# Where the squares go in a pairwise-product kernel: difference-0 products in the shared tiles, 32 separate products of difference 32, and a q sum that accumulates onto a copy

## The chip, the cores and the metric

The kernel runs on one core of one Trainium2 chip. The metric is the device time of one execution in microseconds (us). All arithmetic is float32.

## The reference, cut to what matters

x has 1024 batch rows, 64 fields and 16 embedding columns. Three layers each multiply every field of x with every row of a running h, and contract the 64 x 64 products with weights:

```python
x0 = h = x; xs = []
for i in range(3):
    z = einsum('bfe,bge->bfge', x0, h).reshape(B, 64 * 64, 16)
    y = einsum('oc,bce->boe', W[i], z) + b[i]          # 128 outputs
    x_i, h = (y[:, :64], y[:, 64:]) if i < 2 else (y, y)
    xs.append(x_i)
out = sum(concat(xs, 1), axis=2) @ fc_w.T + fc_b       # (1024, 1)
```

In layer 0 h is x itself, so the products are symmetric. Only pooled sums leave layers 1 and 2. The kernel therefore forms from the unordered products x_f x_g two results of 64 rows each: h (the lower half of layer 0's output) and q (a weight combination that the kernel derives from W1, W2 and fc). The output is the sum over embedding columns of h times q, plus terms linear in x.

## The kernel before, in words

The batch is cut into 32 chunks of 32 rows; a chunk is 64 fields x 512 columns (32 rows x 16). TensorE contracts tiles of 128 products x 512 columns against 64 weight columns, so that a matmul fills one half of the array's columns ("128*64" in the profile) and two of them, one in each column half, run side by side. A float32 matmul of the program is two MATMUL records in the trace, called two passes here.

The unordered products of a chunk fill 16 tiles of 128 rows. With 16 tiles there are 2048 products. Before, these are the differences g - f = 1 to 32 (modulo 64); each product of difference 32 then occurs twice and half of them get weight zero. The 64 squares are not in the tiles. They are in a tile `e` of 128 rows per chunk: x in its upper half (a load, `load_e`), x squared in its lower half (ScalarE, `square`). From it come four more matmuls for a chunk pair's two q sums and two h sums and two for the linear term y:

- `q_extra` (L585): 128 rows, weights `va` or `vb` (linear term above, squares below), one for each chunk.
- `h_extra` (L589): 64 rows (the squares) against `w0ds`, one for each chunk.
- `v0x` (L596): 64 rows (x) against `v0`, one for each chunk.

Six chunks are done plainly at the start and the end. The other 26 form 13 pairs (chunks a and b of pair k). A pair needs 7 instead of 8 contractions of 8 tiles per half because sums and differences of the tiles are formed on VectorE and GpSimd first (`w_product`, `w_both`, `w_mix`; tiles X, T2, T3, B21, B22) and combined weights `ws` are used: 56 matmuls for a pair. Their sums lie in PSUM tiles `alpha`, `beta`, `gamma`, `delta` of 512 columns; each uses one half of the partitions (`p["A"]` or `p["O"]`). `alpha` holds first the common part p1, of which `snap_p1` (L682, ScalarE) keeps a copy in SBUF, and goes on to h and q parts. `w_qa` (L696, VectorE) adds that copy to the separately summed `beta`; `w_hb`, `w_ha`, `w_uu` then form h times q, one half of the partitions at a time.

The order of the work is written out by hand: `at(when, fn)` records a job under a nominal time, the jobs are sorted by it, and each engine executes its own in that order. One nominal unit stands for two matmuls side by side (a slot). A pair's window is 31 units long (`SPAN`). Odd windows (`a_leads`, L807) and even ones (`o_leads`, L821) alternate; a window's `window(...)` zips two columns of jobs, one for each half of the array's columns. `first_window` is the first pair's. In odd windows `joint_squares` (L747) issues all h and y extras of two pairs as eight 64-row matmuls, which occupy the four quarters of the array ("64*64"); the two `q_extra` of a pair stand in the zipped columns (`first_fill`, `late_run`). `end_pair` records VectorE's closing work. The last two chunks, 2 and 3, are contracted in two cuts of 384 and 128 columns (`end_q`, `end_extra`).

SyncE issues the loads in the same order (`load_pair`). Copies into the two PSUM banks tagged `y` (`second`, L568, ScalarE) feed VectorE's products, bank by bank in turn.

Of the kernel before, what the change touches and what calls it, by code (L numbers as in the profile page):

```python
# [42 lines left out]
F = 64  # L43
# [15 lines left out]
NV = 196  # L59
SQ = slice(96, 128)  # L60
# [10 lines left out]
def cin_kernel(ctx, tc, xra, xrb, wh, w0r, w1h, w2t, wx1, wx0, vec, lin, out):  # L71
# [7 lines left out]
    halves = [slice(0, F), slice(F, 128)]  # L79

# [23 lines left out]
    fcb, w0ds, fcr = vs[:, 3:4], vs[:, 4:68], vs[:, 68:196]  # L104

    misc = ps.tile([128, N], F32, tag="acc", name="misc", bufs=4)
# [22 lines left out]
    va, vb, v0 = (const_tile(n, [128, F]) for n in ("va", "vb", "v0"))  # L129
# [6 lines left out]
    xas, xbs, xxs, es = {}, {}, {}, {}  # L136
# [22 lines left out]
    def load_e(c):  # L159
        es[c] = sp.tile([128, N], F32, tag="e", name=f"e_{c}", bufs=4)  # L160
        nc.sync.dma_start(out=es[c][halves[0]], in_=xra[c, 0:F])

    def load_xx(k):
        xxs[k] = sp.tile([128, N], F32, tag="xx", name=f"xx_{k}")
        for n in range(2):
            nc.sync.dma_start(out=xxs[k][halves[n]], in_=xra[2 * k + n, 0:F])

    def copy_x(c):
        k, h, x = c // 2, halves[c % 2], xas[c][:, 0, :]
        if k not in xxs:  # L170
            xxs[k] = sp.tile([128, N], F32, tag="xx", name=f"xx_{k}")
        es[c] = sp.tile([128, N], F32, tag="e", name=f"e_{c}", bufs=4)
        nc.scalar.activation(es[c][halves[1]], x[halves[1]], AF.Square)
        nc.scalar.copy(es[c][halves[0]], x[halves[0]])
        nc.scalar.copy(xxs[k][h], x[h])

    def square(c):
        nc.scalar.activation(es[c][halves[1]], es[c][halves[0]], AF.Square)
# [32 lines left out]
    def shifted(c, j, tag):  # L211
        xbs.setdefault(c, {})[j] = ps.tile(
            [128, N], F32, tag=tag, name=f"xp_{c}_{j}", bufs=4 if tag == "acc" else 2
        )

    def shift_pair(c, js):
        for r, j in enumerate(js):
            for h in range(2):
                at = 4 * (j + 1) + 16 * h
# [5 lines left out]
    w0p = ps.tile([128, 2, NJ, F], F32, tag="set", name="w0p")  # L225
# [9 lines left out]
    def new_acc(c, n=N, tag="acc"):  # L235
        accs[c] = ps.tile([128, n], F32, tag=tag, name=f"acc_{c}", bufs=4 if tag == "acc" else 2)
# [127 lines left out]
    for n in range(2):  # L364
        pv = ps.tile([128, 512], F32, tag=("set", "y")[n], name=f"pv2_{n}")
# [13 lines left out]
    for h in range(2):  # L379
# [10 lines left out]
        ps.tile([128, N], F32, tag=tag, name=f"pm_{m}", bufs=4 if tag == "acc" else 2)  # L390
# [12 lines left out]
    pcx = ps.tile([128, 1], F32, tag="acc", name="pcx", bufs=4)  # L403
# [33 lines left out]
    xb2 = ps.tile([128, N], F32, tag="set", name=f"xp_{c2}_{NJ - 1}")  # L437
    nc.scalar.copy(xb2, xbs[c2][NJ - 1])
    xbs[c2][NJ - 1] = xb2
    for j in (0, 1):  # L440
        xb3 = ps.tile([128, N], F32, tag="y", name=f"xp_{c3}_{j}")
        nc.scalar.copy(xb3, xbs[c3][j])
        xbs[c3][j] = xb3
# [17 lines left out]
    ms = flat(msb).rearrange("p (v t g) -> p v t g", v=2, g=F)  # L461

# [8 lines left out]
    def read_columns(j, queue, half):  # L471
        queue.dma_start(
            out=ms[halves[half], 1, j * NI : (j + 1) * NI],
            in_=skewed(0, 16 * half + 4 * (j + 1), [[row, NI], [1, F]]),
        )

    def read_rows(js, queue, half):
# [3 lines left out]
                16 * half + 4 * (js.start + 1), 0, [[4 * row, js.stop - js.start], [1, NI * F]]  # L481
# [19 lines left out]
    nc.sync.dma_start(out=va[halves[1]], in_=m_ap(0, 0, [[row + F, F], [1, F]]))  # L501
# [56 lines left out]
    def place(v, out, scale):  # L558
        for m in range(2):
            nc.scalar.activation(  # L560
                out[halves[0], 32 * m : 32 * m + 32],
                shift[halves[m], 32 * v : 32 * v + 32], AF.Identity, scale=scale,
            )


    def second(c, j):
        bank = ps.tile([128, N], F32, tag="y", name=f"xp_{c}_{j}")
        nc.scalar.copy(bank, xbs[c][j])  # L568
        xbs[c][j] = bank
# [13 lines left out]
    def new_y(k, tag):  # L583
        ys[k] = ps.tile([128, N], F32, tag=tag, name=f"y_{k}", bufs=4 if tag == "acc" else 2)

    def v0x(c, tag):
        if c // 2 not in ys:
            new_y(c // 2, tag)
        mm(ys[c // 2][halves[c % 2]], v0[halves[0]], es[c][halves[0]], start=True, stop=True)  # L589
# [22 lines left out]
    def w_bank(p, name, tag, bufs):  # L612
        if name not in p:
            p[name] = ps.tile([128, N], F32, tag=tag, name=f"{name}_{p['k']}", bufs=bufs)
        return p[name]

    def alpha(p):
        return w_bank(p, "alpha", "acc", 4)[p["A"]]

    def delta(p):  # L620
        return w_bank(p, "delta", "acc", 4)[p["O"]]

    def gamma(p):
        return w_bank(p, "alpha", "acc", 4)[p["O"]]

    def beta(p):
        return w_bank(p, "beta", "set", 2)[p["O"]]
# [53 lines left out]
    def snap_p1(p):  # L681
        nc.scalar.copy(snaps[0][p["O"]], alpha(p))  # L682
# [4 lines left out]
    def snap_p7(p):  # L687
        nc.scalar.copy(snaps[2][p["A"]], delta(p))  # L688

    def w_hb(p):  # L690
        hb_ = snaps[2][p["A"]]
        nc.vector.scalar_tensor_tensor(hb_, alpha(p), bh1[p["A"]], hb_, ALU.add, ALU.add)

    def w_qa(p):
        q = snaps[0][p["O"]]
        nc.vector.tensor_tensor(q, beta(p), q, ALU.add)  # L696

    def w_ha(p):
        nc.vector.tensor_tensor(delta(p), delta(p), snaps[1][p["O"]], ALU.add)

    def w_uu(p, x, out, factor):
        nc.vector.scalar_tensor_tensor(
            uu[p[out], 0], x(p), 1.0 / QS, factor[p[out]], ALU.mult, ALU.mult
# [36 lines left out]
    def first_fill(p):  # L740
        return [(lambda: q_extra(p["a"], va, p["beta"]),)] + p4_run(p)[-LATE : -LATE // 2]
# [4 lines left out]
    def late_run(p, out=alpha, first=0, last=2 * NI):  # L746
        jobs = w_run(p, out, s4, "B22", out is gamma)[first:last]  # L747
        w = va if p["joint"] == 0 else vb
        return jobs if last < 2 * NI else jobs + [(lambda: q_extra(p["b"], w, p["alpha"]),)]

    def squares(p):
        a, b = p["a"], p["b"]
        h_extra(b, p["alpha"])
        h_extra(a, p["delta"])
        v0x(b, "set")
        v0x(a, "set")

    def joint_squares(q, p):
        a, b = q["a"], q["b"]
        h_extra(b, q["delta"], True)  # L760
        h_extra(a, q["delta"])
        v0x(b, "set")
        v0x(a, "set")
        a, b = p["a"], p["b"]
        h_extra(b, p["alpha"])
        h_extra(a, p["delta"])
        mm(p["delta"][p["A"]], v0[halves[0]], es[b][halves[0]], start=True)
        mm(p["alpha"][p["O"]], v0[halves[0]], es[a][halves[0]], start=True)

    def w_hb_squares(p):  # L770
        hb_ = snaps[2][p["A"]]
        nc.vector.tensor_tensor(hb_, p["delta"][p["A"]], hb_, ALU.add)

    def x_v0x_parts(p):
        for name, h in (("alpha", p["O"]), ("delta", p["A"])):
            nc.vector.scalar_tensor_tensor(
                uu[h, 1, :], p[name][h], cx[h], xxs[p["k"]][h], ALU.add, ALU.mult
            )
# [7 lines left out]
    def first_window(t, p, after, left):  # L786
        window(
            t, p,
            p1_run(p, GROUPS) + left[1][:1] + [(q_extra, 4, va)] + w_run(p, alpha, s2, "T2")
            + left[1][1:] + w_run(p, alpha, s1, "T3"),  # L790
            p7_run(p, GROUPS) + left[0][:1] + [(q_extra, 5, va)]
            + w_run(p, beta, wq_all, "B21", True, 2 * NI) + left[0][1:]
            + p1_run(after, FIRST_ROW) + p4_run(p)[:-LATE],
            8, 8, 18,
        )

    def a_leads(t, p, before, after):
        fill = first_fill(before)
        window(
            t, p,  # L800
            p1_run(p, SECOND_ROW, False) + fill[:2] + w_run(p, alpha, s2, "T2", order=FIRST_ROW)
            + fill[2:] + w_run(p, alpha, s2, "T2", order=SECOND_ROW) + second_fill(before)
            + w_run(p, alpha, s1, "T3") + p7_run(after, FIRST_ROW),
            p7_run(p, GROUPS) + late_run(before) + w_run(p, beta, wq_all, "B21", True, 2 * NI)
            + p4_run(p)[:-LATE],
            4, 8, 15,
        )  # L807
        at(t + 16.9, joint_squares, before, p)

    def o_leads(t, p, before, after):  # L810
        last = after is None
# [5 lines left out]
            + w_run(p, beta, wq_all, "B21", True, 2 * NI)  # L817
            + (late_run(p, gamma, 0, NI) if last else p1_run(after, FIRST_ROW))
            + p4_run(p)[:-LATE],
            8, 4, 19,  # L820
        )  # L821
        if last:
            at(t + 30.2, squares, p)

    def end_pair(t, p, whens):
        hb_, qa, uub, ha, uua, xv, add = whens
        at(t + hb_, w_hb, p)
        at(t + qa, w_qa, p)
        at(t + uub, w_uu, p, alpha, "A", snaps[2])
        at(t + ha, w_ha, p)  # L830
        at(t + uua, w_uu, p, delta, "O", snaps[0])
        if p["joint"] == 0:
# [338 lines left out]
```

## Time and profile before

| | |
|---|---|
| time, three runs | 445.15, 445.06, 444.47 us; median 445.06 us |
| profiled execution, span from first to last instruction | 443.4 us |
| difference of the median to that span | 1.7 us |
| TensorE (PE) busy | 439.8 us, 99% of the span |
| VectorE (DVE) busy | 401.4 us, 91% |
| GpSimd (POOL) busy | 371.9 us, 84% |
| ScalarE (ACT) busy | 117.7 us, 27% |
| granted TensorE clock | 1.000 |

The span is that of the profiled execution; a time of its own beside the span is not recorded, so the 1.7 us that lie around it are taken from the median of the timed runs. In the views, an engine's row names line, operation, output<-inputs, shape (rows*columns of the array, then the moving tile) and count. A PE busy row can hold overlapping matmuls.

### The profile page before, as it was taken

To read this page: it belongs to the slowest core of one execution; us is meant where nothing else is said; L and a number is where in the kernel's file an instruction comes from. 1 tells how busy PE (TensorE), PEld (TensorE's weight loads), DVE (VectorE), ACT (ScalarE), POOL (GpSimd) and SP (SyncE) were. 2 spreads that over 40 slices of the span, in tenths; PEclk is the share of its full clock that TensorE was granted. 3 is DMA by queue.
4 is the path that set the end of the run, shared out by engine and by line. 5 is a ranking of instruction groups with operands and counts; after the bars stand their busy time and mean duration, and the time that the engine had idled before them with its cause. 6 is when DMAs were issued, how large, how long until landed. Compare 5 with 4: busy or idle time off the path is not lost.

```text
span 443.4 us, 5939 instructions
## 1 busy us (share of the span) xinstructions
PE 439.8 (99%) x2228; PEld 159.0 (36%) x2228; DVE 401.4 (91%) x305; ACT 117.7 (27%) x216; POOL 371.9 (84%) x136
## 2 busy tenths in 40 slices
PE   9999999999999999999999999999999999999997
PEld 6333333336633333333333333333333333333345
DVE  4896799998998999999999999999999999999744
ACT  3155341232412123131312214131231313123211
POOL 5823898999998979899798979989798997989900
PEclk9999999999999999999999999999999999999999
DMA  8997997399769756895849868598567958592400
GB/s 283 404 373 193 359 409 290 125 324 232 269 130 342 170 189 232 179 347 119 288 145 260 268 153 307 121 313 210 182 234 186 346 119 282 189 265 71 95 1 0
DMA packets 35220, 99.86 MB, mean 225 GB/s; under 512 B 6420, under 2 KB 7220, under 8 KB 28728
## 3 DMA queue, kind: packets, MB, share of 16 engines
q1 hardware_dynamic: 31784, 84.67, 53.5%
q0 software_dynamic: 1872, 13.63, 16.8%
q10 hardware_dynamic: 1536, 1.18, 1.0%
q8 instruction: 17, 0.28, 0.3%
q14 instruction: 11, 0.09, 0.1%
HBM read 84.20 MB, written 1.64 MB: 194 GB/s over the span
## 4 chain that ended last, share of the span: by engine, by line
PE 94%; DMA 4%; SPq 1%; issue 0%; DVE 0%
PE alpha L540 43%; PE delta L540 23%; PE beta L540 11%; PE acc L540 7%; PE acc L250 4%; PE q L540 3%; DMA z<-in_w1h 3%; PE acc L283 3%; DMA z<-in_w0r 1%; SPq L143 1%; PE y L540 0%; SPq L193 0%; PE pm L396 0%; PE hx L540 0%; PE po L958 0%
## 5 line engine op out<-in xcount | busy, mean ns | idle before, releaser
L671 POOL TENSOR_TENSOR z<-z,z 128x2048 f32<-128x2048 f32 (+1 forms) x85 | 300.1, 3574 | 24.9 <-PE alpha L540 14.3
L654 DVE TENSOR_TENSOR z<-xa,xp 128x2048 f32<-128x2048 f32 x103 | 231.3, 2280 | 3.4 <-ACT xp L568 1.9
L540 PE MATMUL alpha<-z,ws 128*64 128x512 f32 x624 | 233.3, 593 | 0.0
L540 PEld LDWEIGHTS alpha<-z,ws 128*64 128x64 f32 x624 | 74.5, 137 | 89.4 <-issue 82.7
L540 PE MATMUL delta<-z,w_all 128*64 128x512 f32 x208 | 96.4, 592 | 0.0
L540 PE MATMUL alpha<-z,w_all 128*64 128x512 f32 x208 | 92.4, 592 | 0.0
L540 PE MATMUL beta<-z,w_all 128*64 128x512 f32 x208 | 91.7, 593 | 0.0
L540 PE MATMUL delta<-z,ws 128*64 128x512 f32 x208 | 91.4, 592 | 0.0
L568 ACT COPY xp<-xb 128x512 f32<-128x512 f32 x88 | 51.3, 585 | 128.5 <-DVE z L654 111.9
L242 DVE TENSOR_TENSOR z<-xa,xp 128x2048 f32<-128x2048 f32 (+2 forms) x29 | 43.3, 1546 | 2.6 <-ACT xp L568 1.7
L540 PEld LDWEIGHTS alpha<-z,w_all 128*64 128x64 f32 x208 | 28.5, 137 | 29.1 <-issue 27.7
L540 PEld LDWEIGHTS delta<-z,w_all 128*64 128x64 f32 x208 | 28.5, 137 | 28.7 <-issue 27.4
L540 PEld LDWEIGHTS delta<-z,ws 128*64 128x64 f32 x208 | 28.5, 137 | 28.6 <-issue 27.4
L540 PEld LDWEIGHTS beta<-z,w_all 128*64 128x64 f32 x208 | 28.0, 137 | 27.4 <-issue 25.7
L242 POOL TENSOR_TENSOR z<-xa,xb 128x2048 f32<-128x2048 f32 x6 | 27.3, 4569 | 11.1 <-DMA xb<-in_xrb 11.0
L540 PE MATMUL acc<-z,w_all 128*64 128x512 f32 x128 | 28.1, 592 | 0.0
L685 ACT ACTIVATE snap<-alpha,vs 64x512 f32<-64x512 f32 x13 | 8.9, 684 | 52.8 <-PE alpha L540 52.8
L250 PE MATMUL acc<-z,w_all 128*64 128x512 f32 x96 | 21.4, 596 | 0.0
L307 DVE TENSOR_REDUCE acc<-uu 128x64 f32<-128x1024 f32 (+2 forms) x19 | 19.6, 1036 | 0.2
L688 ACT COPY snap<-delta 64x512 f32<-64x512 f32 x13 | 7.5, 580 | 42.2 <-PE alpha L540 27.7
L660 DVE TENSOR_TENSOR xp<-xp,xb 128x512 f32<-128x512 f32 x26 | 18.1, 697 | 0.6
L242 POOL TENSOR_TENSOR z<-xa,xb_gps 128x512 f32<-128x512 f32 (+1 forms) x6 | 14.1, 2369 | 5.3 <-ACT xb_gps L321 4.4
(129 smaller groups left out, 368.4 us busy)
## 6 DMA issues: line engine op xcount, KB each, us to landing
xa<-in_xra SPq DMA_DIRECT2D x32, 1024.0 KB, 5.8
xb<-in_xrb SPq DMA_DIRECT2D x128, 256.0 KB, 7.6
z<-z POOLq DMA_DIRECT2D x13, 1024.0 KB, 8.1
e<-in_xra SPq DMA_DIRECT2D x28, 128.0 KB, 7.2
xx<-in_xra SPq DMA_DIRECT2D x28, 128.0 KB, 2.5
z<-in_w2t SPq DMA_DIRECT2D x2, 1024.0 KB, 11.9
z<-in_wx SPq DMA_DIRECT2D x2, 1024.0 KB, 9.9
xa<-in_xra SPq DMA_DIRECT2D x4, 256.0 KB
```

The lines of the kernel that those rows point to most:

```text
L143: queue.dma_start(out=xas[c][rows * n : rows * (n + 1), at, :], in_=bass.AP(tensor=xra.tensor, offset=c * XR * N + (at.start + rows * n) * ...
L242: engine.tensor_tensor(blocks[zs[c, j]][:, at, :], xas[c][:, at, :], xbs[c][j].unsqueeze(1).to_broadcast([128, last - first, N]), ALU.mult,)
L250: nc.tensor.matmul(accs[c][halves[i % 2]], w_all[:, j * NI + i, 0:64], blocks[zs[c, j]][:, i, :], start=(j == 0 and i < 2), stop=(j == las ...
L283: nc.tensor.matmul(accs[c][halves[1 - c % 2]], w_all[:, t, 64:128], blocks[zs[c, j]][:, i, :], start=(t == 0), stop=False, skip_group_chec ...
L307: nc.vector.tensor_reduce(acc[rows, of, k, half], uu[rows, of if at is None else at, E * half.start : E * half.stop].rearrange("p k (b e) ...
L540: nc.tensor.matmul(out, w, rhs, start=start, stop=stop, skip_group_check=True)
L568: nc.scalar.copy(bank, xbs[c][j])
L654: engine.tensor_tensor(blocks[b], xas[c], xbs[c][j].unsqueeze(1).to_broadcast([128, NI, N]), ALU.mult)
L660: nc.vector.tensor_tensor(bank, bank, xbs[p["b"]][j], ALU.add)
L671: nc.gpsimd.tensor_tensor(*(blocks[b][:, first:last] for b in (o, x, y)), ALU.subtract if in1 == "T3" else ALU.add,)
L685: nc.scalar.activation(snaps[1][p["O"]], alpha(p), AF.Identity, bias=bh1[p["A"]])
L688: nc.scalar.copy(snaps[2][p["A"]], delta(p))
```

## The change

Tiles now cover differences 0 to 31, so the squares are ordinary rows of the 16 tiles (the index of the second factor is smaller by one). Left over are the 32 products of difference 32. For a pair of chunks they are formed by one load of two shifted copies of x (`load_d`, tiles `xs` and `d`, four transfers of 128 KB in place of two for `e`), a ScalarE copy into a `y` bank (`far_bank`) and one VectorE product (`far_product`). Each is a matmul of 32 rows (`far`; tiles of 32 x 64 of the array), two per chunk: one for q and one for h. The linear part of q is a matmul of 64 rows (`along_x`). `w0ds`, `va`, `vb` and the squares go; `dh`, `dq`, `dqh`, `v1` come.

`beta` becomes the other half of `alpha`'s bank: `snap_p1` copies p1 there (PSUM to PSUM), and the cross products accumulate onto the copy (`start` False). `w_qa` goes, and `w_uu` takes both halves of the partitions in one instruction. PSUM banks are assigned by name (`bank`, `pair_bank`) instead of in turn by tag.

```diff
-    def load_e(c):
...
-    def square(c):
-        nc.scalar.activation(es[c][halves[1]], es[c][halves[0]], AF.Square)
+    def load_d(k):
+        for kept, name, first in ((xss, "xs", 0), (ds, "d", 32)):
+            for n in range(2):
+                nc.sync.dma_start(out=pair_tile(kept, name, k)[halves[1 - n]],
+                    in_=xra[2 * k + n, first : first + F])
+    def far_bank(k):
+        xbs["d", k] = bank(f"d_{k}", "y")
+        nc.scalar.copy(xbs["d", k], ds[k])
+    def far_product(k):
+        nc.vector.tensor_tensor(ds[k], xbs["d", k], xss[k], ALU.mult)
...
-    def q_extra(c, w, out=None):
-        out = accs[c][halves[1 - c % 2]] if out is None else out[halves[c % 2]]
-        mm(out, w, es[c])
-    def h_extra(c, out=None, start=False):
-        out = accs[c] if out is None else out
-        mm(out[halves[c % 2]], w0ds[halves[1]], es[c][halves[1]], start=start)
+    def along_x(c, out, cols=slice(0, N), turned=0):
+        h = halves[c % 2 ^ turned]
+        mm(out, v1[h], (xss if turned else xxs)[c // 2][h, cols])
+    def far(c, w, n, out, cols=slice(0, N), start=False):
+        r = quarter_of(c, n)           # 32 rows
+        mm(out, w[r], ds[c // 2][r, cols], start=start)
...
     def snap_p1(p):
-        nc.scalar.copy(snaps[0][p["O"]], alpha(p))
+        nc.scalar.copy(beta(p), alpha(p))
-    def w_qa(p):
...
-    def w_uu(p, x, out, factor):
...
+    def w_uu(p):
+        nc.vector.scalar_tensor_tensor(
+            uu[:, 0], p["alpha"], 1.0 / QS, p["hs"], ALU.mult, ALU.mult)
...
-    def joint_squares(q, p):
...
+    def q_extras(p):
+        a, b = p["a"], p["b"]
+        along_x(b, alpha(p))
+        along_x(a, beta(p))
+        far(b, dqh, 0, alpha(p))
+        far(a, dq, 0, beta(p))
+    def h_extras(p):
+        far(p["b"], dh, 1, alpha(p))
+        far(p["a"], dh, 1, delta(p))
+    def extras(q, p, both):
+        if q is not None:
+            q_extras(q)
+        h_extras(p)
+        if both:
+            for r in (q, p):
+                ys[r["k"]] = pair_bank(r, "y")
+                v0x(r["k"], int(r is p))
...
     def first_window(t, p, ...):
...
+        at(t + 21.9, extras, None, p, False)
     def a_leads(t, p, ...):
...
-        at(t + 16.9, joint_squares, before, p)
+        at(t + 15.9, extras, before, p, True)
     def o_leads(t, p, ...):
...
+        at(t + 19.9, extras, before, p, False)
...
-    for c in (0, 1, 4, 5):
-        at(28.1, v0x, c, "acc")
-        at(28.1, h_extra, c, None, c < 2)
-    zipped(30, [(q_extra, 0, va)], [(q_extra, 1, va)])
+    at(24.1, v0x, 0)
+    at(24.1, v0x, 2, 1)
+    at(29.1, plain_extras)             # 4 along_x, 8 far
...
+    at(t + 19.9, end_extras, 0)        # 2 along_x, 2 far, 384 columns
+    at(t - 0.7, end_v0x)               # 4 v0x
+    at(t + 6.9, end_pair_extras)       # q_extras of the last pair, 2 far for h
+    at(t + 15.9, end_extras, 1)        # (t of the second cut) 128 columns
```

In the code after, `v0x(k)` issues both chunks' matmuls of a pair. `load_d` stands at t - 8 of a window, `far_bank` at t + 4.3 and `far_product` at t + 6.9.

More of the change, by code (lines that the diff above doesn't have):

```diff
@@ L79, in cin_kernel, with bank, quarter_of @@
     halves = [slice(0, F), slice(F, 128)]
+    turns = {"acc": [0, 1, 2, 3], "set": [4, 5], "y": [6, 7]}
+    def bank(name, where, shape=(128, N)):
+        if isinstance(where, str):
+            n = turns[where].pop(0)
+            turns[where].append(n)
+        else:
+            n = where
+        return ps.tile(list(shape), F32, tag=f"bank{n}", name=name, bufs=1)
+    def quarter_of(c, n):
+        first = 32 * (2 * (1 - c % 2) + n)
+        return slice(first, first + 32)
     def const_tile(name, shape):
@@ L103, in cin_kernel @@
     fc2, bh1, bh2 = vs[:, 0:1], vs[:, 1:2], vs[0:64, 2:3]
-    fcb, w0ds, fcr = vs[:, 3:4], vs[:, 4:68], vs[:, 68:196]
-    misc = ps.tile([128, N], F32, tag="acc", name="misc", bufs=4)
+    fcb, fcr = vs[:, 3:4], vs[:, 68:196]
+    misc = bank("misc", "acc")
     zeros = nc.const_aps.tensor(0.0, [128, 128])
@@ L211, in shifted @@
     def shifted(c, j, tag):
-        xbs.setdefault(c, {})[j] = ps.tile(
-            [128, N], F32, tag=tag, name=f"xp_{c}_{j}", bufs=4 if tag == "acc" else 2
-        )
+        xbs.setdefault(c, {})[j] = bank(f"xp_{c}_{j}", tag)
     def shift_pair(c, js):
@@ L223, in shift_pair @@
                 )
-    w0p = ps.tile([128, 2, NJ, F], F32, tag="set", name="w0p")
+    w0p = bank("w0p", "set", (128, 2, NJ, F))
     for j, tag in ((1, "y"), (0, "acc"), (2, "set"), (3, "acc")):
@@ L235, in new_acc @@
     def new_acc(c, n=N, tag="acc"):
-        accs[c] = ps.tile([128, n], F32, tag=tag, name=f"acc_{c}", bufs=4 if tag == "acc" else 2)
+        accs[c] = bank(f"acc_{c}", tag, (128, n))
     def product(c, j, first=0, last=NI, engine=nc.vector, uses=1):
@@ L364, in cin_kernel @@
     for n in range(2):
-        pv = ps.tile([128, 512], F32, tag=("set", "y")[n], name=f"pv2_{n}")
+        pv = bank(f"pv2_{n}", ("set", "y")[n])
         for k in range(4):
@@ L389, in cin_kernel @@
     pms = [
-        ps.tile([128, N], F32, tag=tag, name=f"pm_{m}", bufs=4 if tag == "acc" else 2)
+        bank(f"pm_{m}", tag)
         for m, tag in enumerate(("acc", "set", "y", "y"))
@@ L402, in cin_kernel @@
     cx = const_tile("cx", [128, 1])
-    pcx = ps.tile([128, 1], F32, tag="acc", name="pcx", bufs=4)
+    pcx = bank("pcx", "acc", (128, 1))
     for to in halves:
@@ L435, in cin_kernel @@
     used(mb)
-    xb2 = ps.tile([128, N], F32, tag="set", name=f"xp_{c2}_{NJ - 1}")
+    xb2 = bank(f"xp_{c2}_{NJ - 1}", "set")
     nc.scalar.copy(xb2, xbs[c2][NJ - 1])
@@ L440, in cin_kernel @@
     for j in (0, 1):
-        xb3 = ps.tile([128, N], F32, tag="y", name=f"xp_{c3}_{j}")
+        xb3 = bank(f"xp_{c3}_{j}", "y")
         nc.scalar.copy(xb3, xbs[c3][j])
@@ L480, in read_rows @@
             in_=skewed(
[L481 removed]
+                16 * half + 4 * js.start + 3, 0, [[4 * row, js.stop - js.start], [1, NI * F]]
             ),
@@ L559, in place @@
         for m in range(2):
[L560 to L563, printed above, removed]
+            for h in halves:
+                nc.scalar.activation(
+                    out[h, 32 * m : 32 * m + 32],
+                    shift[halves[m], 32 * v : 32 * v + 32], AF.Identity, scale=scale,
+                )
     def second(c, j):
-        bank = ps.tile([128, N], F32, tag="y", name=f"xp_{c}_{j}")
-        nc.scalar.copy(bank, xbs[c][j])
-        xbs[c][j] = bank
+        out = bank(f"xp_{c}_{j}", "y")
+        nc.scalar.copy(out, xbs[c][j])
+        xbs[c][j] = out
     def plain_product(when, c, j):
@@ L573, in plain_product, with new_y, v0x, plain_extras @@
         at(when, product, c, j, uses=NI)
[L575 to L589 removed]
+    def along_x(c, out, cols=slice(0, N), turned=0):
[4 more added lines that the diff above has]
+        mm(out, w[r], ds[c // 2][r, cols], start=start)
+    def new_y(k, where):
+        ys[k] = bank(f"y_{k}", where)
+    def v0x(k, turned=0):
+        x = (xss if turned else xxs)[k]
+        for n in range(2):
+            mm(ys[k][halves[n ^ turned]], v0[halves[n]], x[halves[n]], start=True, stop=True)
+    def plain_extras():
+        for c in (0, 1, 4, 5):
+            along_x(c, accs[c][halves[1 - c % 2]], turned=c // 4)
+        for k in (0, 2):
+            for c in (2 * k, 2 * k + 1):
+                far(c, dq, k // 2, accs[c][halves[1 - c % 2]])
+                far(c, dh, 1 - k // 2, accs[c][halves[c % 2]], start=k == 0)
     def contract(c, j, i, start=False):
@@ L746, in late_run @@
     def late_run(p, out=alpha, first=0, last=2 * NI):
[L747 to L751, printed above, removed]
+        return w_run(p, out, s4, "B22", out is gamma)[first:last]
+    def q_extras(p):
         a, b = p["a"], p["b"]
[L753 to L756, printed above, removed]
-    def joint_squares(q, p):
[L759 to L778, printed above, removed]
+        along_x(b, alpha(p))
[13 more added lines that the diff above has]
+                v0x(r["k"], int(r is p))
     def window(t, p, a_column, o_column, p1, p7, u2):
@@ L992, in new_ends @@
             ends.append(
-                ps.tile([128, cols.stop - cols.start], F32, tag="acc", name=f"q_{n}", bufs=4)
+                bank(f"q_{n}", (ROLES["three"][2], ROLES["odd"])[n], (128, cols.stop - cols.start))
             )
@@ L1002, in end_q, with end_extras, end_v0x, end_pair_extras @@
         used(z, 0.5)
-    def end_extra(c, n):
-        mm(ends[n][halves[1 - c % 2]], va, es[c][:, cuts[n]])
-    def end_squares():
-        hx = ps.tile([128, N], F32, tag="y", name="hx")
+    def end_extras(n):
+        for c in (2, 3):
+            along_x(c, ends[n][halves[1 - c % 2]], cuts[n])
+        for c in (2, 3):
+            far(c, dq, 0, ends[n][halves[1 - c % 2]], cuts[n])
+    def end_v0x():
+        for k, where in ((q["k"], ROLES["three"][0]), (1, "y")):
+            new_y(k, where)
+            v0x(k, int(k == 1))
+    def end_pair_extras():
+        hx = bank("hx", "y")
         hxs.append(hx)
+        q_extras(q)
         for c in (2, 3):
-            h_extra(c, hx, True)
-            v0x(c, "y")
+            far(c, dh, 1, hx[halves[c % 2]], start=True)
     def end_h():
@@ L1086, in cin_kernel @@
     pool(1, 2, 1, rows=turned, start=False, stop=True)
-    pl = ps.tile([2, N - E * CUT], F32, tag="acc", name="pl", bufs=4)
+    pl = bank("pl", ROLES["three"][1], (2, N - E * CUT))
     nc.tensor.matmul(pl, ones, uu[:, 1, last], start=True, stop=False)
```

204 lines of the change are left out of this document (111 added, 93 removed).

## The prediction

> **What bounds the kernel now.** I read the page first, then the waits of PE.
>
> ```profile
> span 443.4 us, 5939 instructions
> ...
> PE 439.8 (99%) x2228; PEld 159.0 (36%) x2228; DVE 401.4 (91%) x305; ACT 117.7 (27%) x216; POOL 371.9 (84%) x136
> ...
> PE 94%; DMA 4%; SPq 1%; issue 0%; DVE 0%
> ```
>
> ```profile
> PE misc L110 <- PEq L1160: 0.8, 1, 0.8
> PE pm L396 <- DMA z<-in_w1h: 0.4, 1, 0.4
> ```
>
> The third line of the page is the chain that ended last: 94% of it is PE. The two lines behind are all that PE waited for in the whole run, 1.2 us, both at the start. So PE's own queue sets the end, and any work taken off VectorE, ScalarE or SyncE is worth nothing by itself. The steady part says the same. Two windows, one odd and one even, make a period; one is shown by the table of stretches (stretch, length, then busy time and count of PE, weight loads, DVE, ACT and POOL, clock, DMA share, GB/s):
>
> ```profile
> 122.10:173.91 51.81, 51.81 (x249) 17.09 (x248) 49.68 (x37) 11.94 (x21) 47.23 (x16) 1.00 0.73 223
> ```
>
> PE is busy for all 51.81 us, DVE for 49.68 us, POOL for 47.23 us. I therefore count what PE issues: slots, and changes of the array's shape. The timeline of PE at the extras gives both prices (start, duration, operation, shape):
>
> ```profile
> 173.39 0.59 PE L540 MATMUL alpha<-e,va 128*64 128x512 f32 x1
> 173.91 0.65 PE L540 MATMUL delta<-e,vs 64*64 64x512 f32 x2
> 173.93 0.65 PE L540 MATMUL y<-e,v 64*64 64x512 f32 x2
> 174.39 0.60 PE L540 MATMUL delta<-e,vs 64*64 64x512 f32 x2
> ...
> 174.82 0.59 PE L540 MATMUL delta<-e,vs 64*64 64x512 f32 x1
> ...
> 175.25 0.59 PE L540 MATMUL delta<-e,vs 64*64 64x512 f32 x1
> ...
> 175.79 0.64 PE L540 MATMUL alpha<-z,ws 128*64 128x512 f32 x1
> ...
> 176.27 0.59 PE L540 MATMUL alpha<-z,ws 128*64 128x512 f32 x1
> ```
>
> *A slot.* From 174.39 to 174.82 to 175.25 the step from one pass to the next is 0.43 us. A matmul is two passes, so a slot costs 0.86 us. At 173.91 and 173.93 two and two 64-row matmuls start together: four quarters of the array cost one slot. What counts is how many slots the order fills, not how many rows work.
>
> *A change of shape.* Going in, the two steps 173.39 to 173.91 and 173.91 to 174.39 take 0.52 + 0.48 = 1.00 us instead of 0.86: 0.14 us lost. Going out, 175.25 to 175.79 to 176.27 takes 1.02 us: 0.16 us lost. I take 0.15 us each. A period has 58 slots of 128 rows, 2 of 64 and two changes: (51.81 - 2 x 0.86 - 0.30) / 58 = 0.86 us, so 128 rows cost the same as 64.
>
> The Trainium skill, in "TensorEngine Tiling (Array Packing)", section "Tiling Modes", says that a change of the tiling mode, unlike a change of the tile, drains the engine. By that rule work of two shapes never overlaps; the trace agrees as far as it goes, with the 0.52 us step, and the rule speaks against this change, which brings a third shape. A sum in which shapes overlap is the first rival.
>
> **The extras' slots.** Before, by the view of the tile e (two passes for each matmul):
>
> ```profile
> L540 PE MATMUL y<-e,v x40: 589/589/641, 79.5 to 419.7; 64*64 64x512 f32 x40
> L540 PE MATMUL delta<-e,vs x38: 589/589/640, 122.1 to 418.9; 64*64 64x512 f32 x38
> L540 PE MATMUL beta<-e,va x26: 592/592/593, 110.6 to 425.3; 128*64 128x512 f32 x26
> L540 PE MATMUL alpha<-e,vs x14: 589/589/640, 123.0 to 418.9; 64*64 64x512 f32 x14
> L540 PE MATMUL alpha<-e,vb x14: 592/592/592, 144.6 to 428.7; 128*64 128x512 f32 x14
> L540 PE MATMUL alpha<-e,va x12: 592/592/592, 121.1 to 380.6; 128*64 128x512 f32 x12
> L540 PE MATMUL alpha<-e,v x12: 589/589/589, 123.0 to 382.5; 64*64 64x512 f32 x12
> L540 PE MATMUL delta<-e,v x12: 589/589/589, 123.0 to 382.5; 64*64 64x512 f32 x12
> L540 PE MATMUL acc<-e,vs x8: 589/589/640, 79.5 to 80.9; 64*64 64x512 f32 x8
> L540 PE MATMUL acc<-e,va x8: 592/592/644, 81.4 to 92.2; 128*64 128x512 f32 x8
> L540 PE MATMUL q<-e,va x8: 272/380/486, 434.9 to 439.9; 128*64 128x384 f32 x4, 128*64 128x128 f32 x4
> L540 PE MATMUL hx<-e,vs x4: 589/589/589, 419.3 to 419.7; 64*64 64x512 f32 x4
> ```
>
> The 64-row rows sum to 128 passes, 64 matmuls, four to a slot: 16 slots. The 128-row rows of full length sum to 60 passes, 30 matmuls, two to a slot: 15 slots; the four in cuts of 384 and 128 columns make one more. Together 32 slots. They stand in 8 blocks of 64-row work (one plain, six of joint_squares, the last pair's), which is 16 changes of shape.
>
> After, the order of the jobs gives:
>
> - `v0x`: 32 matmuls of 64 rows, four at a time, 8 slots (one plain, six odd windows, one at the end).
> - `along_x`: 34 of 64 rows. Four plain ones share a slot. The rest come two at a time, `along_x(b)` and `along_x(a)`, on two of the four quarters: 13 pairs, 13 slots, and the two cuts make one. 15 slots.
> - `far`: 66 of 32 rows. The plain eight lie on eight different tiles of the array, one slot. Each of the 12 windows behind the first has four (two of q for the pair before, two of h for its own), on four different 32-row groups: 12 slots. The first window's two, the end's four, and the cuts take one slot each: 3. Together 16 slots.
>
> That is 39 slots against 32: **7 more, 7 x 0.86 = 6.0 us.** In a period: 60 slots before; after it 56 + 3 (odd: along, far, v0x) + 2 (even: along, far) = 61. The 17 slots of `q_extra` that go are more than paid for by narrow matmuls that leave most of the array idle.
>
> **The changes of shape.** `extras` in an odd window runs 128 -> 64 -> 32 -> 64 -> 128 rows, 4 changes; in an even one 128 -> 64 -> 32 -> 128, 3. Six of each: 42. Plain part 2 + 3, first window 2, end 2 + 3, the cuts 3 + 2 (the second goes straight on to the pooling matmuls): 17. So 59 against 16: **43 more, 43 x 0.15 = 6.5 us.** No row shows a change between 64 and 32 rows; 22 of the 43 are of that kind. From below they could cost nothing, which leaves 21 x 0.15 = 3.2 us; from above I double them, 22 x 0.30 + 3.2 = 9.8 us. I take 0.15, the measured change nearest to it. None could gain: before and after a change, a pass can at best follow the one in front by the same 0.43 us.
>
> **Work on the other engines.** It stays beside PE, with these checks.
>
> ```profile
> L654 DVE TENSOR_TENSOR z<-xa,xp 128x2048 f32<-128x2048 f32 x103 | 231.3, 2280 | 3.4 <-ACT xp L568 1.9 <-POOL z L671 0.2
> ...
> L696 DVE TENSOR_TENSOR snap<-beta,snap 64x512 f32<-64x512 f32 x13 | 8.9, 685 | 9.9 <-PE beta L540 9.9
> ...
> L682 ACT COPY snap<-alpha 64x512 f32<-64x512 f32 x13 | 7.5, 580 | 40.3 <-PE delta L540 21.7 <-PE alpha L540 18.6
> ```
>
> - DVE loses `w_qa` (13 x 0.685 us and the 9.9 us of waiting in front of it) and the second half of `w_uu`; it gains 16 `far_product` of the same 512 columns, 0.69 us by the same row. It gets lighter, worth nothing to the time. PE waits for `far_product`, but that stands at t + 6.9 and its matmuls at t + 15.9 or later: 9 slots, 7.7 us of cover for 0.69 us and a ScalarE copy of 0.58 us.
> - `snap_p1` must now be finished before PE adds cross products to `beta`. In even windows p1 ends with slot 8 and the cross products start with slot 12; T2, which already waited for that read, starts with slot 10. Cover: two slots, 1.7 us, for a copy of 0.58 us. Behind a late copy PE's whole queue would stand.
> - `load_d` issues four transfers instead of two and, on SP's queue, waits until PE has read the `d` of two pairs before (slot 16 to 22 of the window before). Behind it stand the next pair's loads; their first product is due at t + 9.6, some 18 slots, 15 us, after that wait ends.
> - GpSimd's added copies and sums lie in the head and are small; weight and mix steps are unchanged.
>
> One place is tight. `v0x` of the plain part moves 4 units up, and 3 slots fewer precede it:
>
> ```profile
> 76.67 0.47 ACT L560 ACTIVATE v<-shift 64x32 f32<-64x32 f32 x2 [3.81 <-DVE shift L555]
> ```
>
> ```profile
> 79.52 0.64 PE L540 MATMUL y<-e,v 64*64 64x512 f32 x1
> ```
>
> PE would come to it at 79.52 - 3 x 0.86 = 76.9 us. Its weights were placed at 77.1 us; after, one product (2.28 us) moves behind them, two `far_product` (1.4 us) and two more placements (0.5 us) come in front: 76.7 us at best, later if a `y` bank hands over late. I allow 0 to 1.5 us in the range and 0 in the sum.
>
> **The sum.** 443.4 + 6.0 + 6.5 = 455.9 us of span; the median lies 1.7 us above the profiled span, so **457.6 us**. This case's own range, from 3.2 to 9.8 us for the changes and 0 to 1.5 us of stall: 454.3 to 462.4 us.
>
> **The rivals.**
>
> *Shapes overlap (faster).* `along_x` lies on two opposite quarters and the `far` of the same block on tiles of the other two. If a 32-row matmul may start while 64-row ones run, an even window's extras take 1 slot, an odd one's 2, and a period 59. Over the kernel the extras fall from 32 slots to 25 (6 even and 12 odd, plain part 3, first window 1, end 3), -6.0 us, and only changes between 128 and fewer rows cost: 38 against 16, +3.3 us. 445.1 - 2.7 = 442.4 us. It decides from the first window on. For it: the tiles are disjoint. Against: at every change in the trace the first pass starts 0.52 us after the last one, though inside a shape the next pass follows by 0.43. Chance 0.10. The Trainium skill, same page, section "Restrictions and Gotchas", says that different row tiles must not write the same PSUM bank at once; `along_x(b)` and the q `far` of b both write `alpha`, so by it those two could not overlap. No row here shows it.
>
> *Four 32-row matmuls don't run at once (slower still).* If two row groups in the same column half take turns, the 12 windows' blocks and the end's cost one slot more each and the plain eight up to 3: 16 x 0.86 = 13.8 us, 471.4 us. For it: no 32-row form is in the trace. Against: of the four 64-row matmuls at 173.91, two row groups in each column half run together. Chance 0.09.
>
> *A new wait.* The ScalarE copy into `beta`, or a bank handed over late, stops PE in each pair. The third row above has ScalarE idle for 40.3 us in front of its 13 copies, waiting for others, so a copy can queue behind a blocked one; at one copy, 0.58 us, for 13 pairs this is 7.5 us, 465.1 us. Against: ScalarE is busy for 27% of the span, and the slack above is two slots. Chance 0.09.
>
> **How the numbers follow.** My forecast has 0.70, the rivals 0.10, 0.09 and 0.09; 0.02 is left for costs and gains that cancel. Faster by over 0.2% (what a measurement of this kernel can tell from no change) is the first rival, 0.10; same 0.02; slower 0.88. The range of 8 in 10 takes the forecast's own range, some room below it, and reaches up past the new wait: 452.5 to 466.
>
> **What would show it.** In the profile after: a period of 53.4 us (51.81 + 0.86 + 5 x 0.15) instead of 51.81; 32*64 passes starting four at a time, 0.43 us apart, and never before the 64*64 passes in front of them are 0.4 us old; steps of 0.5 us at each change of shape; no waits of PE behind the head. DVE busy for less of a period. I am wrong if 32*64 and 64*64 passes start within 0.05 us of each other (first rival), if the 32*64 block takes 1.7 us (second), or if the waits of PE name ScalarE or VectorE in every pair (third).

## The result, and the profile after

The changed kernel takes 458.91 us (median of 4 runs, 458.77 to 460.81) against 444.76 us: ratio 1.0324, 95% interval 1.03 to 1.0349. The profiled execution is the longest of the four; the same kernel, profiled again as `again` below, has a span of 457.0 us, and sums over the whole span are made against that one.

The head of the page after, and all waits of PE:

```profile
span 459.0 us, 6156 instructions
...
PE 454.2 (99%) x2296; PEld 159.2 (35%) x2296; DVE 386.0 (84%) x282; ACT 111.8 (24%) x206; POOL 377.4 (82%) x143
```

```profile
PE misc L123 <- PEq L1209: 0.8, 1, 0.8
PE y L576 <- ACT v L597: 0.5, 1, 0.5
```

PE is as full as before, with 68 matmul records more, and VectorE is 15 us lighter. One period in the table of stretches, with the columns as before:

```profile
123.48:176.91 53.43, 53.43 (x258) 17.01 (x257) 46.32 (x32) 11.38 (x20) 47.46 (x16) 1.00 0.75 226
```

53.43 us against 51.81; the forecast was 53.4. Of the five periods of this execution three are that long, and two are longer, 53.58 us and this one:

```profile
230.34:284.37 54.03, 54.03 (x258) 19.83 (x256) 47.25 (x33) 11.44 (x20) 47.47 (x16) 1.00 0.74 224
```

In `again` all five lie between 53.43 and 53.54 us. The block of extras of an odd window in PE's timeline:

```profile
122.95 0.59 PE L576 MATMUL delta<-z,w_all 128*64 128x512 f32 x1
...
123.48 1.07 PE L576 MATMUL alpha<-xx,v 64*64 64x512 f32 x4
124.48 0.64 PE L576 MATMUL alpha<-d,dqh 32*64 32x512 f32 x1
124.49 0.64 PE L576 MATMUL alpha<-d,dq 32*64 32x512 f32 x1
124.50 0.64 PE L576 MATMUL alpha<-d,dh 32*64 32x512 f32 x1
124.50 0.64 PE L576 MATMUL delta<-d,dh 32*64 32x512 f32 x1
124.96 0.59 PE L576 MATMUL alpha<-d,dqh 32*64 32x512 f32 x1
...
125.50 0.65 PE L576 MATMUL y<-xx,v 64*64 64x512 f32 x2
...
125.98 0.60 PE L576 MATMUL y<-xx,v 64*64 64x512 f32 x2
...
126.52 0.64 PE L576 MATMUL alpha<-z,ws 128*64 128x512 f32 x1
...
127.00 0.59 PE L576 MATMUL alpha<-z,ws 128*64 128x512 f32 x1
```

Four 32-row matmuls start within 0.02 us of each other, and their second pass follows 0.48 us later. Going back to 64 rows, the two steps 124.96 to 125.50 to 125.98 take 0.54 + 0.48 = 1.02 us, so this change costs 1.02 - 0.86 = 0.16 us, and 126.52 and 127.00 say the same of the way to 128. The whole block, 122.95 to 127.00, is 8 steps and 4 changes: (4.05 - 8 x 0.43) / 4 = 0.15 us a change. No pass of one shape starts beside a pass of another. The Trainium skill ("TensorEngine Tiling (Array Packing)", section "Tiling Modes") says that a change of the tiling mode drains the engine; the trace agrees. The page gives no price; in this block it is 0.14 to 0.16 us.

### The profile page after: what moved, and what is told of

Same layout as the page of the kernel before. It is cut to its first block, busy times and chain, and to the rows that moved or that the text cites. A ratio compares the mean times of both kernels' runs of the same rounds, so it can differ in the third digit from the quotient of the medians.

```text
span 459.0 us, 6156 instructions
## 1 busy us (share of the span) xinstructions
PE 454.2 (99%) x2296; PEld 159.2 (35%) x2296; DVE 386.0 (84%) x282; ACT 111.8 (24%) x206; POOL 377.4 (82%) x143
## 4 chain that ended last, share of the span: by engine, by line
PE 82%; DMA 9%; DVE 4%; issue 2%; SPq 1%; ACT 0%; ACTq 0%; DVEq 0%
PE alpha L576 52%; PE delta L576 22%; PE q L576 4%; DMA z<-in_w2t 2%; DMA xa<-in_xra 2%; PE y L576 2%; PE acc L576 2%; DMA xb<-in_xrb 2%; DVE z L271 2%; DMA z<-in_w0r 1%; DVE z L713 1%; DMA z<-md 1%; DMA md<-z 1%; PE gamma L576 1%; SPq L455 1%
## 5 line engine op out<-in xcount | busy, mean ns | idle before, releaser
L576 PE MATMUL alpha<-z,ws 128*64 128x512 f32 x616 | 229.3, 593 | 0.0
L576 PE MATMUL alpha<-z,w_all 128*64 128x512 f32 x416 | 184.8, 594 | 0.0
L576 PEld LDWEIGHTS alpha<-z,ws 128*64 128x64 f32 x616 | 71.7, 137 | 82.8 <-issue 80.5
L576 PEld LDWEIGHTS alpha<-z,w_all 128*64 128x64 f32 x416 | 55.8, 137 | 55.7 <-issue 51.2
L751 DVE SCALAR_TENSOR_TENSOR snap<-alpha,vs,snap 64x512 f32<-64x512 f32 x13 | 9.7, 747 | 11.2 <-PE alpha L576 11.1
L205 DVE TENSOR_TENSOR d<-d,xs 128x512 f32<-128x512 f32 x16 | 11.0, 685 | 9.7 <-ACT d L202 9.7
```

The source lines that it names most:

```text
L205: nc.vector.tensor_tensor(ds[k], xbs["d", k], xss[k], ALU.mult)
L576: nc.tensor.matmul(out, w, rhs, start=start, stop=stop, skip_group_check=True)
```

## The experiments

**`again`** is the changed kernel once more, beside the first three: 458.74 us (458.19 to 460.51), ratio 1.0324 (1.0303 to 1.0345). In its timeline five of the six stretches from an odd to an even block of extras take 30.66 or 30.67 us, and one takes 30.77; those from an even to an odd block all take 22.77 or 22.78. So of its loss about 0.1 us lies in waits inside these windows.

**`no_far_in_windows`** prices the 32-row slots. It leaves out the `far` matmuls of the 13 windows.

```diff
-            q_extras(q)
-        h_extras(p)
+            along_x(q["b"], alpha(q))
+            along_x(q["a"], beta(q))
```

> Leaves out the 32-row matmuls of the 13 windows (difference 32 of those pairs is missing from h and q); load, copy and product of difference 32 stay. Slot theory: 13 slots x 0.86 = 11.2 us and 20 changes x 0.15 = 3.0 us less than the changed kernel: 444.7 us, a period of 59 slots and 4 changes, 51.2 us. Wait theory: the waits that hang on far_product go, those on the copy onto beta and on the transfer stay; the gain need not be that sum, 450 us or more.

Measured 444.03 us (443.18 to 444.87), ratio 0.9986 (0.9977 to 0.9994). Against `again` the `far` of the windows cost 458.74 - 444.03 = 14.7 us, where the price list has 14.2, and about what the whole change costs.

**`no_far_no_along`** takes `along_x` out as well (neither `q_extras` nor `h_extras` is called in `extras`).

> Leaves out, in the 13 windows, the matmuls of the far products and those along x (only the four v0x of every other window are left of the extras). By slots alone: 25 slots of 0.86 us and 32 changes of shape of 0.15 us fewer than the changed kernel, 458.7 - 21.5 - 4.8 = 432.4 us. Rival: a period of 49.2 us would leave the other engines' limits 1.7 us away (GpSimd 47.5, VectorE 47.2 a period): if they or the accumulating transfer decide, 434 to 440.

Measured 431.73 us (431.3 to 431.83), ratio 0.9703 (0.969 to 0.9716). Again the slots and changes give the time, within 0.7 us. At this pace neither VectorE nor GpSimd sets the end.

**`two_more_products`** gives VectorE work back.

```diff
     def far_product(k):
+        if k > 3:
+            for n in range(2):
+                nc.vector.tensor_tensor(uu[:, 1], xbs["d", k], xss[k], ALU.mult)
         nc.vector.tensor_tensor(ds[k], xbs["d", k], xss[k], ALU.mult)
```

> The changed kernel with two more 128x512 products on VectorE for each pair (1.4 us a pair, 2.7 us in a period of 53.4, of which VectorE is busy 47.2 now; 49.9 is what it was before the change). If VectorE's relief is worth nothing, as predicted: 458.7 within 0.5. If VectorE decides, or the relief paid for part of the slots: 461 or more (13 x 1.4 = 18 us at the most).

Measured 458.06 us (457.79 to 458.35), ratio 1.0297 (1.0283 to 1.0311), just under the range of the first case. VectorE is busy for 401.5 us, as much as before the change (401.4), and the time does not rise. Its relief was worth nothing.

**`v0_beside_along`** uses the two idle quarters: `v0x` of the pair before runs beside its `along_x` in every window, which saves one slot and one change in each period.

```diff
-            q_extras(q)
+            along_x(q["b"], alpha(q))
+            along_x(q["a"], beta(q))
+            new_y(q["k"], ROLES["three"][0]) if q["k"] == 14 else ys.update({q["k"]: pair_bank(q, "y")})
+            v0x(q["k"], 1)
+            far(q["b"], dqh, 0, alpha(q))
+            far(q["a"], dq, 0, beta(q))
...
-        if both:
-            for r in (q, p):
-                ys[r["k"]] = pair_bank(r, "y")
-                v0x(r["k"], int(r is p))
...
-                end_pair(t, q, (0.7, 22.3, 22.4, 17.8, 36))
+                end_pair(t, q, (0.7, 22.3, 22.4, 22.2, 36))
```

> v0x of a pair is issued in the window behind it, directly after the pair's two along_x, on the two quarters that these leave idle; nothing is left out. Odd windows lose one slot and one change of shape (128, 64, 32, 128 rows), even windows keep theirs. Slot theory: 6 slots x 0.86 + 6 changes x 0.15 = 6.1 us less than the changed kernel, 452.8 us, 60 slots and 6 changes in a period, 52.4 us. Wait theory: the same matmuls wait for the same things, so no gain beyond 1 us: 458 us.

Measured 458.79 us (457.13 to 459.72), ratio 1.0311 (1.029 to 1.0331): a miss by 6 us. The blocks shrank as priced, but between the odd and the even block PE and its weight loads now wait. Of the waits of the weight loads, and the period that shows it best:

```profile
PEld alpha L576 <- POOL z L730: 5.7, 9, 0.8
PEld delta L576 <- DMA z<-z: 4.7, 6, 1.3
```

```profile
228.11:282.04 53.93, 53.51 (x258) 16.93 (x257) 47.25 (x33) 11.44 (x20) 47.48 (x16) 1.00 0.74 224
```

The transfer `z<-z` is `w_mix`'s: GpSimd's queue adds one tile onto another by a DMA, 1 MB, for the even window's `delta`. In the timeline the six stretches from the odd to the even block take 30.02 to 31.14 us, and in `v0_beside_along_d_later` below 29.65 to 29.84: 5.6 us in all, nearly the whole miss.

**`v0_before_far`** only reorders the odd block to along, v0x, far, which saves one change of shape.

```diff
-            q_extras(q)
-        h_extras(p)
+            along_x(q["b"], alpha(q))
+            along_x(q["a"], beta(q))
         if both:
             for r in (q, p):
                 ys[r["k"]] = pair_bank(r, "y")
                 v0x(r["k"], int(r is p))
+        if q is not None:
+            far(q["b"], dqh, 0, alpha(q))
+            far(q["a"], dq, 0, beta(q))
+        h_extras(p)
```

> In odd windows the order along, far, v0x becomes along, v0x, far; nothing is left out. The slots stay (v0x of the pair in front needs the quarters of along_x), and one change of shape in each of six windows goes. Slot theory: 6 x 0.15 = 0.9 us less than the changed kernel, 458.0 us; if changes between 64 and 32 rows cost nothing, 0.0 us less. Wait theory: 0.0 us, or a loss where far now comes late for its sums.

Measured 461.36 us (460.34 to 461.79), ratio 1.0369 (1.0355 to 1.0384), a miss the other way. The block is 0.16 us shorter, but the weight loads wait six times for the same transfer:

```profile
PEld delta L576 <- DMA z<-z: 3.4, 6, 1.0
```

The six stretches from the odd to the even block are together 3.9 us longer than 6 x 30.66 us, though each holds the shorter block. That the late transfer is the reason fits this; the move of `load_d` below was not tried in this order. The transfer's issue to landing in one odd window, from the DMA view of before, of the changed kernel and of `v0_beside_along` (last column us):

```profile
z<-z POOLq DMA_DIRECT2D x1, 1024.0 KB, 8.1
```

```profile
z<-z POOLq DMA_DIRECT2D x1, 1024.0 KB, 14.4
```

```profile
z<-z POOLq DMA_DIRECT2D x1, 1024.0 KB, 14.3
```

What runs beside it stands in SyncE's waits and timeline, here of the changed kernel, with the transfer's own row from GpSimd's timeline between:

```profile
SPq L185 <- PE alpha L576: 127.4, 12, 14.3
```

```profile
236.69 0.84 POOL L728 DMA_DIRECT2D z<-z  x1
```

```profile
222.38 0.47 SPq L185 DMA_DIRECT2D xs<-in_xra  x1
232.47 1.11 SPq L185 DMA_DIRECT2D d<-in_xra  x2
233.67 0.53 SPq L157 DMA_DIRECT2D xa<-in_xra  x1
...
238.51 0.33 SPq L157 DMA_DIRECT2D xa<-in_xra  x1
238.94 4.36 SPq L171 DMA_DIRECT2D xb<-in_xrb  x6
```

`load_d` (L185) issues nothing for 9.6 us, until the block at 230.34 has read the old `d`. Behind it the two chunk loads of 1 MB leave 4.8 us apart, around the accumulating transfer. Before they left 7.3 us apart, both behind it (234.26 and 241.51, transfer at 231.17).

**`d_loads_later`** and **`v0_beside_along_d_later`** test this by one number, in the changed kernel and in `v0_beside_along`.

```diff
-        at(t - 8 if early else t + 1, load_d, p["k"])
+        at(t - 2.9 if early else t + 1, load_d, p["k"])
```

> The changed kernel with one moved call: the four 128 KB loads of a pair's x and its copy 32 elements on are put in SyncE's queue behind the next pair's first chunk load (t-2.9 in place of t-8). Theory A (the queue): in the changed kernel SyncE stands 127.4 us in 12 waits for TensorE's matmuls on 'alpha' to free these tiles, and the chunk loads stand behind them, so they meet the accumulating transfer of GpSimd's queue, which lands after 13 to 14.4 us in odd windows against 8.1 before, and TensorE's next matmuls wait for it. Then here the odd transfers land within 8 to 10 us, the steps of 0.55 us at about 251 and of 0.53 at about 305 are gone, and the time is 457.2 to 458.3 (span 455.5 to 456.7). Theory B (the slots alone): the meeting is harmless in this kernel, 458.7 within 0.4, whatever the landing. Theory C (the loads come too late now): VectorE's product for the far matmuls waits at t+6.9 and holds its queue, 459.5 or more.

> v0_beside_along (458.8 us where its slots gave 452.8) with the same moved call. Theory A (the queue of SyncE delays the chunk loads into the accumulating transfer, and that ate the gain): TensorE's waits for that transfer (4.7 us in 6) and for GpSimd behind it (5.7 us in 9) shrink to under 2 us together, odd transfers land within 10 us, and the time is 453 to 455. Theory B (GpSimd's own work, 47.5 us of a period, or the order of its queue bounds this kernel): the landing may shorten but the time stays above 457.

`d_loads_later` took 458.54 us (458.32 to 460.13), ratio 1.0315 (1.0299 to 1.0332): unchanged, theory B. `v0_beside_along_d_later` took 452.01 us (451.68 to 452.86), ratio 1.0164 (1.015 to 1.0178): theory A, 6.8 us less than without the move, and 1 us below the range given. In both the odd transfer is quick again (8.4 us in the first; below, the second, with a period of it), and the chunk loads are 7.2 us apart in its timeline of SyncE, both behind the transfer:

```profile
z<-z POOLq DMA_DIRECT2D x1, 1024.0 KB, 8.5
```

```profile
227.55:279.99 52.44, 52.44 (x259) 16.74 (x257) 47.24 (x33) 11.36 (x20) 47.50 (x16) 1.00 0.75 231
```

```profile
233.86 0.86 POOL L728 DMA_DIRECT2D z<-z  x1
```

```profile
229.98 1.19 SPq L185 DMA_DIRECT2D d<-in_xra  x2
...
235.59 0.33 SPq L157 DMA_DIRECT2D xa<-in_xra  x1
...
242.83 0.33 SPq L157 DMA_DIRECT2D xa<-in_xra  x1
```

The period is the 52.4 us of the price list. The last odd window is an exception in both kernels: there the transfer still lands after 13.2 and 13.0 us. Four `xb` loads of 256 KB, 1 MB together, leave ahead of it in place of a chunk load.

The weight loads' waits for the transfer are gone, but not those for GpSimd, which theory A also had shrink:

```profile
PEld alpha L576 <- POOL z L730: 4.9, 6, 0.8
```

With these the period is as priced, so they cost nothing. So the late transfer costs next to nothing in the slower order (0.75 us in the two long periods of the first profile, 0.1 us in `again`) and almost 7 us in the quicker one. Other loads move with `load_d` too; which of them matters most was not tried.

**`copy_part_alone`** puts only the last part of the change into the kernel before, for the pairs of every other window.

```diff
+        if p["joint"] == 0:
+            p["beta"] = p["alpha"]
...
-        nc.scalar.copy(snaps[0][p["O"]], alpha(p))
+        nc.scalar.copy(beta(p) if p["joint"] == 0 else snaps[0][p["O"]], alpha(p))
...
     def w_qa(p):
+        if p["joint"] == 0:
+            return
...
-        w_run(p, beta, wq_all, "B21", True, 2 * NI)
+        w_run(p, beta, wq_all, "B21", p["joint"] > 0, 2 * NI)
```

In these pairs `w_ha` also writes its sum to SBUF, where `w_uu` then reads it.

> The kernel before with the last part of the change alone, for the pairs of every other window: ScalarE copies the q sum at T2's start into the other half of its bank, TensorE goes on adding the wq matmuls of B21 there without start, and VectorE's addition of the two banks (w_qa) is dropped. If it is free, as predicted (ScalarE's copy takes 0.46 us and TensorE's first matmul on that half comes slots later): the time of before within 0.5 us, 444.4 to 445.4. If TensorE waits for the copy: up to 0.5 us in each of 6 windows, 446 to 448. If VectorE's relief (0.7 us for each of these pairs) is worth something: under 444.

Measured 449.98 us (449.48 to 450.06), ratio 1.0111 (1.0094 to 1.0128): 5.0 us, more than any of the three theories gave. PE's waits and the timeline have the place:

```profile
PE alpha L540 <- ACT snap L687: 3.9, 5, 0.8
```

```profile
150.01 0.59 PE L540 MATMUL alpha<-z,ws 128*64 128x512 f32 x1
...
150.65 0.68 ACT L687 ACTIVATE snap<-alpha,vs 64x512 f32<-64x512 f32 x1 [4.21 <-PE alpha L540]
...
151.39 0.64 PE L540 MATMUL alpha<-z,w_all 128*64 128x512 f32 x1 [0.79 <-ACT snap L687]
```

It is not the copy: that takes 0.56 us in the trace, not 0.46, and PE never waits for it. `snap_u2` reads one half of `alpha` at 150.65; the cross products on the other half now lie in the same PSUM tile, and the last two of them are held until it is done: a step of 1.38 us instead of 0.43, 0.95 us in each of 5 windows. The period grows from 51.81 to 52.82 us, five times 1.0 us, which is the whole loss. The Trainium skill ("PSUM — Partial Sum Buffer", section "PSUM bank collisions raise a hardware error") lets two engines use different quadrants of one bank at once and calls guarding by the whole bank the simple version. The read and the matmuls use different halves, so the wait may be such a guard and no need of the chip. No experiment here lets the two overlap, so this stays open.

**`copy_part_reordered`** and **`cross_in_one_piece`** try the reason from both sides. In `o_leads` the change has `cross[:-2] + lead[:2] + cross[-2:] + lead[2:]`, so that two matmuls of the next pair stand where the read falls. The first run adds this order to `copy_part_alone`; the second takes it out of the changed kernel:

```diff
-            + cross[:-2] + lead[:2] + cross[-2:] + lead[2:] + p4_run(p)[:-LATE],
+            + cross + lead + p4_run(p)[:-LATE],
```

> copy_part_alone with the change's order of one column as well: in the windows where a ScalarE read of 'alpha' falls between TensorE's cross products on the other half of that bank, the last two cross products (two slots) come behind the first two matmuls of the next pair's p1. Theory A (the shared bank makes the last cross products wait for that read, 0.95 us a window, 5 windows, and that is all that the copy costs): the wait goes, the time is that of before within 0.6 us, 444.4 to 445.6. Theory B (the copy itself, or VectorE's freed time, moves something else): 447 or more.

> The changed kernel with that order undone: the eight cross products of these windows in one piece, the next pair's p1 behind them. Theory A: TensorE waits for ScalarE's read in 5 or 6 windows, 0.95 us each: 458.7 + 4.8 to 5.7 = 463.5 to 464.4. Theory B: no wait, 458.7 within 0.6.

445.58 us (445.13 to 446.36), ratio 1.0022 (1.0013 to 1.0031), and 465.15 us (464.25 to 465.83), ratio 1.0455 (1.044 to 1.047). What is left of PE's waits for that read in the one and in the other:

```profile
PE alpha L540 <- ACT snap L687: 0.8, 1, 0.8
```

```profile
PE alpha L576 <- ACT snap L744: 4.7, 6, 0.8
```

In the first the five waits are gone. The one that is left (at 410.81, with 0.95 us of time) is a new one, in the last window, whose pair keeps its separate `beta`. There the two matmuls moved forward are `gamma`'s, which in this kernel lie in the other half of that pair's `alpha` tile: the same wait once more. In the second all six windows wait, and odd to even block takes 31.67 us instead of 30.66: 6 x 1.0 us, of the 6.4 us measured. That is 0.75 us above theory A's range, which counted 0.95 us a window and not 1.0; the last 0.3 us remain unexplained. The accumulation onto the copy is free only in the order that came with it.

No kernel with the new products in full beats the kernel before; the best of them, `v0_beside_along_d_later`, is 1.6% behind it.

## Why the prediction was right, point by point

- *Slots and changes of shape.* Right, in the mechanism and in the number. The period came out as summed, and leaving out `far`, then `along_x`, gave 444.0 and 431.7 us where the same prices gave 444.7 and 432.4. The 22 changes between 64 and 32 rows, for which no row existed, cost what the others cost. *Shapes overlap* and *four 32-row matmuls don't run at once* are both refuted by the block shown above. The rule on one PSUM bank that the prediction quotes from the Trainium skill does not hold here as it is worded: at 124.48 and 124.49 matmuls of different row groups (weights `dqh` and `dq`) write the two halves of one `alpha` bank together. Two small readings were off without moving the sum: `q_extra` filled 16 slots by the prediction's own count, not 17, and the second 32-row pass follows the first by 0.48 us, not 0.43, part of the price of the change in front of it.
- *The sum* was 1.1 us short: span 457.0 in `again`, 455.9 forecast. The missed term is mostly at the very end. Before, the last output is issued at 441.29 and the span ends at 443.4, 2.1 us later. In the two profiles of the changed kernel and in `d_loads_later` it is 3.0 us each (453.97 to 457.0 in `again`), and in the other kernels built on the changed one 2.3 to 2.7 us. What makes it longer was not found.
- *The plain part's `v0x`.* Right in kind: PE waits 0.5 us there for the placed weights in the first profile and not at all in `again`, within the 0 to 1.5 us kept for it and left out of the sum.
- *DVE gets lighter, worth nothing.* Right, by `two_more_products`.
- *`load_d` on SP's queue.* This step failed, and it was luck that the time did not show it. It looked only at when the loads behind it are due. It did not ask what they would run into: `z<-z` lands 6 us later in odd windows. In the changed kernel the move of `load_d` is worth 0.2 us (458.54 against 458.74, not to be told apart); in the next better order it is 6.8 us.
- *`snap_p1`, and the rival of a new wait.* The copy is covered, as said. But the step looked at the wrong ScalarE instruction. The danger of the shared bank was `snap_u2`, whose read stops the matmuls on the other half, 6.4 us over the kernel. The rival priced a stop at one copy in each of 13 pairs, 7.5 us; the stop that exists is one of 1.0 us in 6 of them. It is avoided by the moved `lead` matmuls, a line of the change that the prediction had not costed, so on this point, too, the time owes something to luck.

## What to carry to other kernels

Where TensorE sets the end, count its slots and its changes of array shape, and treat a narrow matmul as a full slot unless others really share it. When a transfer is put on a queue, ask what the transfers behind it will then collide with, and check that again when the critical engine gets quicker: slack that hides a late transfer goes with the first improvement. When two results are put in one PSUM bank, list every read of either half, not only the new one.

## What the runs showed of the hardware

- Passes of 64 and of 128 rows step by 0.43 us at 512 columns of float32. The 32-row blocks here are two passes long, 0.48 us apart, as the first two 64-row passes behind a change are (125.50 to 125.98). Up to eight 32-row matmuls share a pass (plain part of the changed kernel, all starting between 83.75 and 83.80). A change of shape costs 0.14 to 0.18 us; the 0.18 is that block's way out (84.23 to 84.79 to 85.27).
- An accumulating 1 MB transfer of GpSimd's queue lands after 12.9 to 14.8 us when about 1 MB of SyncE's loads leaves in the 3 us ahead of it and a 1 MB load within 2 us behind it. That is so in the odd windows of the changed kernel, of `again`, `v0_before_far` and `v0_beside_along`, and in the last odd window of the two kernels with `load_d` later. In the other windows behind the first it lands after 6.9 to 9.9 us in these kernels and after 7.7 to 8.6 us before.
